# The odd x product of a block, shared by the block's last four steps

## The chip, the cores and the metric

The kernel runs on one core of a Trainium2 chip. The metric is the device time of one execution in microseconds. Three runs of the kernel before gave a median of 1644.59 us (1644.28 to 1645.88).

## What is computed

A gated recurrent layer runs over 512 time steps with a batch of 8 and 512 units, and its states are added to the input. `h0` is a second input; all numbers are float32. The reference, cut to its core:

```python
def step(h, x_t):
    fused = jax.nn.sigmoid(jnp.concatenate([x_t, h], axis=-1) @ w_W + w_b)
    hidden_state, output_state = jnp.split(fused, 2, axis=-1)
    memory_state = x_t @ wx_W + wx_b + hidden_state * (h @ wh_W + wh_b)
    h_new = output_state * h + (1.0 - output_state) * jnp.tanh(memory_state)
    return (h_new, h_new)
_, hs = jax.lax.scan(step, h0, xT)
return x + jnp.swapaxes(hs, 0, 1)
```

Each step has a part that needs the state h (products with 1536 columns of weights in all) and a part that needs x alone (1536 columns too). The second can be computed for many steps at once, ahead of the recurrence.

## The kernel before

**One step of the recurrence.** The 512 steps are one unrolled loop (L469). The state is kept transposed: 128 partitions by four chunks k of 8 columns, in two halves (chunks 0 and 1, chunks 2 and 3). A step's TensorE work is given by `ORDER` (L27): A0 to A3, D0 to D3, H2 and H3. A letter is a bank of PSUM and a slice of weights, the digit the chunk of h that is the stationary operand. `BANKS` (L31) gives the widths of the moving operand, 256, 128 and 64 columns; for chunks 2 and 3, A has 192 columns only (L485). Each of these is four matmuls (L491), one for each group of 32 columns of the array, so that the four run side by side. Each float32 matmul is recorded as two matmul instructions with a weight load each (two passes): D of one step, 4 chunks by 4 groups, is 32 records.

Behind A, VectorE and ScalarE turn the sums into gates and the new state: `turn_r`, `turn_h`, `turn_z`, `memory`, `update` (L594 to L620), for the first half of h first, and then for the second, which also needs D and H. The scans of `update(1, 0)` and `update(1, 1)` (L619, L620) make chunks 2 and 3 of the new state; the next step's A2 and A3 wait for them, while its A0 and A1 need the first half alone.

**The x part.** After the products of a step, TensorE gets some of the x part (L493 to L500). For the first groups of steps these are plain products. From step 14 on they come from `products` (L376), for blocks c = 2 to 31 of 16 steps each: each block's product of x with the weights is made by a scheme of seven by seven smaller products (after Strassen and Winograd), whose operands are sums that GpSimd (x) and VectorE (weights, once) have made. So a block has 49 products, each with 96 columns (`BL`, L35) and again four matmuls side by side. The seven outer stages are worked through in the order of `STAGES`; of a stage, three products go to bank `xps[0]`, four to bank `xps[1]` (`SLOTS`, L41). When a bank's products of a stage are done, VectorE adds them up with `drain` (L390, recorded as L403), and a next stage's products may only be written to that bank behind it. GpSimd puts the results together (`result`, L405).

`products` is a generator that yields after each product, and `take(later, n)` (L420) lets it run for n yields. 49 products in 16 steps is three in each, and one over: the last step of a block takes four (L500). The steps at which the drains are issued are worked out from the same count (L456 to L463), with a product counted as 1.

Of the kernel before, what the change touches and what calls it, by code (L numbers as in the profile page):

```python
# [14 lines left out]
NQ = 4  # L15
# [19 lines left out]
BL = 96  # L35
# [3 lines left out]
FRESH = (2, 5, 1)  # L39

SLOTS = ((1, 6, 7), (2, 3, 4, 5))  # L41

LEAD = 18

PLAIN = (2, 3, 5, 6, 8, 10, 11, 13, 14, 16)

# [8 lines left out]
def tile_cond_rnn_residual(  # L55
# [144 lines left out]
    xps = [psum.tile([P, 512], F32, name=f"xp{q}") for q in range(2)]  # L200

    def mm(out_, lhsT, rhs, start=False):
        nc.tensor.matmul(  # L203
            out_, lhsT, rhs, start=start, stop=False, skip_group_check=True
        )
# [20 lines left out]
    for b in range(2):  # L226
        c0 = COLS.start + BL * b
# [56 lines left out]
    def wx_of(kh, nh):  # L284
        return wx[:, 2 * kh : 2 * kh + 2, :, HALF * nh : HALF * nh + HALF]
# [31 lines left out]
    def x_block(c, r, kh):  # L317

        return xins[c][:, :, 2 * kh : 2 * kh + 2, 32 * r : 32 * r + 32]
# [31 lines left out]
    def x_sums(c):  # L351
        jobs = [(x_sum, c, n) for n in range(4)]
        return jobs + [(inner_x, c, n, p) for n in range(4) for p in (0, 2, 3)]

    def left(c, p, q):

        xr, kh = {1: (0, 0), 2: (0, 1), 4: (1, 1)}.get(p, (None, None))
        at = {1: 0, 2: 1, 4: 2, 5: 3, 6: 4, 7: 5, 3: 6}[p]
        if q in (3, 5, 6, 7):
            return si[c % 2][:, at, {5: 0, 6: 1, 7: 2, 3: 3}[q]]  # L360
        e, k = {1: (0, 0), 2: (0, 1), 4: (1, 1)}[q]
        if xr is None:
            return so[c % 2][:, at - 3, e, k]
        return x_block(c, xr, kh)[:, e, k]

    def right(p, q, j):

        kh, nh = {1: (0, 0), 2: (1, 0), 3: (1, 1)}.get(p, (None, None))
        at = {1: 0, 2: 1, 3: 2, 5: 3, 6: 4, 7: 5, 4: 6}[p]
        if q > 3:  # L370
            return ti[:, at, {5: 0, 6: 1, 7: 2, 4: 3}[q], j]
        k, b = {1: (0, 0), 2: (1, 0), 3: (1, 1)}[q]
        w = tw[:, at - 3] if kh is None else wx_of(kh, nh)
        return w[:, k, j, BL * b : BL * b + BL]

    def products(c):  # L376

        for q in STAGES:
            for bank in range(2):
                for n, p in enumerate(SLOTS[bank]):  # L380
                    for j in range(NQ):
                        mm(
                            xps[bank][32 * j : 32 * j + 32, BL * n : BL * n + BL],
                            left(c, p, q),
                            right(p, q, j),
                            start=q in FRESH and n == 0,
                        )
                    yield

    def drain(q, bank):  # L390

# [28 lines left out]
    def take(it, n=None):  # L420
        while n is None or n > 0:
            if next(it, it) is it:
                return
            n = None if n is None else n - 1

    def x_side():
        for c in range(2, NCH):
            yield from products(c)
# [4 lines left out]
    later = x_side()  # L433
# [12 lines left out]
    def at_step(i, *todo):  # L446
        jobs.setdefault(i, []).extend(todo)
# [4 lines left out]
    for c in range(2, NCH):  # L452
        w0 = TC * c - LEAD
        for n, q in enumerate(x_sums(c)):
            at_step(w0 - (13 if c > 2 else 10) + n // 2, q)
        done = 0  # L456
        for w in range(TC):
            n = done
            done += 3 + w // 15
            for m, q in enumerate(STAGES):  # L460
                for bank in range(2):
                    if n < 7 * m + 3 + 4 * bank <= done:
                        drains.setdefault(w0 + w, []).append((q, bank))  # L463
        for e, w in ((0, 11), (1, 15)):
            for n in range(7):
                at_step(w0 + w + n // 2, (result, e, n))

    pool_done = {}
    for i in range(T):  # L469
        g, s = divmod(i, GS)  # L470
        c, t = divmod(i, TC)
# [6 lines left out]
        for n in (ORDER if i else FIRST).split():  # L478
# [3 lines left out]
            bank, k = n[0], int(n[1])  # L482
# [10 lines left out]
        if 1 <= i < 4:  # L493
            take(first[2], 2 if i == 3 else 3)
        elif i == 0:
            take(first[1], 1)
        elif i < 4 + len(PLAIN):
            take(first[4], PLAIN[i - 4] - (PLAIN[i - 5] if i > 4 else 0))
        else:
            take(later, 4 if (i + LEAD) % TC == TC - 1 else 3)  # L500

        rows = slice(B * s, B * s + B)
        s1 = (i + 1) % GS
# [255 lines left out]
```

## Time and profile before

| what | value |
|---|---|
| three runs, median | 1644.59 us |
| profiled execution, device time | 1642.24 us |
| profiled execution, span of the trace | 1640.4 us |
| granted TensorE clock, mean | 0.999 |
| busy PE, weight load, VectorE, ScalarE, GpSimd | 99%, 83%, 84%, 60%, 34% of the span |

The span runs from the first to the last instruction of the trace. In the profile PE is TensorE's matmuls, PEld its weight loads, which overlap with them, DVE VectorE, ACT ScalarE and POOL GpSimd. A matmul's end is modelled and overlaps with the next, so that starts say more of TensorE than durations do. All matmuls are issued by one helper and carry its line, L203; they are told apart by the tiles they write (A, D, H, xp). In a timeline, neighbouring instructions of a kind are merged into one row with a count, and the brackets give the idle time of that engine ahead of the row and whose work ended it.

### The profile page before, as it was taken

Reading aid. Unit: us, or ns where it says so; the run is one execution under the profiler, and the core shown is the slowest. Engines: PE = TensorE matmul, PEld = TensorE weight load, DVE = VectorE, ACT = ScalarE, POOL = GpSimd, SP = SyncE. Lnnn points to the kernel's source line nnn. Section 1 sums busy time; section 2 is a strip of 40 time slices with the busy share of each in tenths; the row PEclk is TensorE's granted clock in tenths of the full one; section 3 lists DMA queues with packets and bytes.
Section 4 is the critical chain, followed back from the end, with each engine's and each line's share of the span. In section 5 each row is a group of like instructions: output and inputs, shape, how many; then the busy total and the mean of one; then the engine's idle time right before and its main releaser. Section 6 shows DMA issues by size and latency. Waiting matters only on the chain.

```text
span 1640.4 us, 124811 instructions
## 1 busy us (share of the span) xinstructions
PE 1627.4 (99%) x53006; PEld 1362.0 (83%) x53006; DVE 1384.8 (84%) x11239; ACT 977.2 (60%) x5520; POOL 550.3 (34%) x1443
## 2 busy tenths in 40 slices
PE   8999999999999999999999999999999999999998
PEld 5788888888888888888888888888888888888876
DVE  8888888888888888888888888888888888888886
ACT  3666666666555665666566666566666666556655
POOL 3333333333333333333333333333333333333220
PEclk9999999999999999999999999999999999999999
DMA  4000000000000000000000000000000000000000
GB/s 182 17 5 17 18 18 18 5 18 18 18 17 17 5 18 18 17 18 5 17 18 18 17 10 14 17 18 18 18 5 18 17 18 17 5 17 12 11 11 10
DMA packets 11512, 31.08 MB, mean 19 GB/s; under 512 B 1220, under 2 KB 1732, under 8 KB 10952
## 3 DMA queue, kind: packets, MB, share of 16 engines
q1 hardware_dynamic: 10800, 22.94, 4.1%
q8 instruction: 414, 6.78, 1.7%
q14 instruction: 146, 1.20, 0.2%
q10 hardware_dynamic: 152, 0.16, 0.0%
HBM read 14.70 MB, written 8.39 MB: 14 GB/s over the span
## 4 chain that ended last, share of the span: by engine, by line
PE 97%; DVE 1%; DMA 1%; issue 0%; SPq 0%; ACT 0%; DVEq 0%
PE A L203 48%; PE D L203 26%; PE xp L203 16%; PE H L203 7%; DMA wd<-in_wd_dram 1%; DVE tr L519 0%; DVE m L507 0%; DMA head<-in_xh_dram 0%; DVE md1B L576 0%; DVE md1A L534 0%; DVE tz L519 0%; DVE hT L507 0%; SPq L142 0%; ACT hT L243 0%; DVE idle L542 0%
## 5 line engine op out<-in xcount | busy, mean ns | idle before, releaser
L203 PE MATMUL A<-wa,hT 128*32 128x256 f32 x16352 | 884.7, 356 | 4.1 <-DVE hT L507 4.1
L203 PEld LDWEIGHTS A<-wa,hT 128*32 128x32 f32 x16352 | 509.5, 123 | 236.2 <-DVE hT L507 133.6
L203 PE MATMUL D<-wd,hT 128*32 128x128 f32 x16384 | 543.0, 273 | 1.0 <-DMA wd<-in_wd_dram 1.0
L203 PEld LDWEIGHTS D<-wd,hT 128*32 128x32 f32 x16384 | 482.7, 122 | 21.8 <-DMA wd<-in_wd_dram 1.3
L673 POOL TENSOR_TENSOR ot<-xin,hT 128x32 f32<-128x32 f32 x503 | 136.0, 270 | 1048.4 <-DVE hT L507 1036.9
L243 ACT ACTIVATE hT<-m 128x8 f32<-128x8 f32 x2048 | 324.1, 207 | 91.5 <-DVE m L507 91.3
L243 ACT ACTIVATE md0A<-tr 128x16 f32<-128x16 f32 x512 | 112.8, 220 | 409.5 <-DVE tr L519 409.5
L519 DVE STREAM_TRANSPOSE tr<-A 128x64 f32<-128x64 f32 x511 | 127.7, 250 | 221.1 <-PE A L203 221.0
L243 ACT ACTIVATE hT<-hT 128x16 f32<-128x16 f32 x1024 | 233.3, 228 | 85.0 <-DVE hT L507 84.2
L203 PE MATMUL H<-wa,hT 128*32 128x64 f32 x8208 | 210.5, 219 | 0.0
L203 PEld LDWEIGHTS H<-wa,hT 128*32 128x32 f32 x8208 | 187.8, 122 | 0.1
L507 DVE TENSOR_TENSOR_SCAN hT<-hd0B,hT 128x24 f32<-128x24 f32 x1024 | 154.5, 192 | 21.8
L507 DVE TENSOR_TENSOR_SCAN hT<-hd0A,hT 128x24 f32<-128x24 f32 x1024 | 171.6, 168 | 0.0
L507 DVE TENSOR_TENSOR_SCAN m<-md0B,md1B 128x24 f32<-128x24 f32 x1024 | 154.6, 193 | 0.0
L203 PE MATMUL xp<-ti,si 128*32 128x96 f32 x5040 | 150.0, 246 | 0.0
L507 DVE TENSOR_TENSOR_SCAN m<-md0A,md1A 128x16 f32<-128x16 f32 x1024 | 142.2, 181 | 5.0
L243 ACT ACTIVATE md0B<-tr 128x16 f32<-128x16 f32 x512 | 116.2, 227 | 42.8 <-DVE tr L519 1.3
L418 POOL TENSOR_TENSOR xs<-ff 128x192 f32<-128x192 f32 x240 | 141.0, 599 | 0.0
L576 DVE STREAM_TRANSPOSE md1B<-A 128x64 f32<-128x64 f32 x511 | 130.1, 255 | 0.0
L243 ACT ACTIVATE hd0A<-tz 128x16 f32<-128x16 f32 x512 | 116.5, 228 | 21.5
L534 DVE STREAM_TRANSPOSE md1B<-H 128x64 f32<-128x64 f32 x512 | 128.2, 250 | 0.1
L569 DVE STREAM_TRANSPOSE hd0B<-sz 128x64 f32<-128x64 f32 x512 | 126.3, 247 | 0.0
(103 smaller groups left out, 1919.8 us busy)
## 6 DMA issues: line engine op xcount, KB each, us to landing
xin<-in_x_dram SPq DMA_DIRECT2D x31, 256.0 KB, 3.2
out_dram<-ot SPq DMA_DIRECT2D x31, 256.0 KB, 2.3
wx<-in_wx_dram SPq DMA_DIRECT2D x4, 768.0 KB, 6.9
wa<-in_wa_dram SPq DMA_DIRECT2D x4, 512.0 KB, 9.6
wd<-in_wd_dram SPq DMA_DIRECT2D x1, 768.0 KB
wd<-in_wd_dram SPq DMA_DIRECT2D x1, 256.0 KB, 11.2
out_dram<-ot SPq DMA_DIRECT2D x1, 192.0 KB, 1.9
head<-in_xh_dram ACTq DMA_DIRECT2D x1, 144.0 KB, 4.9
```

The source lines that it names most:

```text
L203: nc.tensor.matmul(out_, lhsT, rhs, start=start, stop=False, skip_group_check=True)
L243: inst = nc.scalar.activation(out_, in_, func, **kw).ins
L418: nc.gpsimd.tensor_tensor(to, a, b, ALU.add)
L507: return nc.vector.tensor_tensor_scan(*[t_[:, :, c_].rearrange("p n c s -> p (n c s)") for t_ in (out_, d0, d1)], 0.0, ALU.mult, ALU.add,).ins
L519: inst = nc.vector.transpose(t_.rearrange("p c n -> p (c n)"), raw[n][hf]).ins
L534: inst = nc.vector.transpose(md1[hf][g % 2][:, :, :, hf].rearrange("p n c -> p c n"), raw["h"][hf]).ins
L569: inst = nc.vector.transpose(hd0[1][i % 2][:, :, :, 2].rearrange("p n c -> p c n"), sz).ins
L576: nc.vector.transpose(md1[1][g % 2][:, :, :, 0].rearrange("p n c -> p c n"), ps["A"][:, :HU])
L673: pool_done[i + 1] = nc.gpsimd.tensor_tensor(ot[:, t], x_of(c, slice(0, NQ), t, 1), hTs[(i + 1) % NH][:, :, :, B * s1 : B * s1 + B, 2].rea ...
```

## The change

The x work of a step is counted in columns, not in products. `BURSTS` gives the columns of a block's 16 steps: 288 (three products) in twelve of them and 312 in the last four. `products` cuts a product at the end of a step's share: it runs the four matmuls on the first columns, yields, and runs them again on the rest in the next step, with the same stationary operand. The drains' steps are worked out in columns, and each step takes one yield.

```diff
+BURSTS = (288,) * 12 + (312,) * 4
...
     def products(c):
+        todo = list(BURSTS)
         for q in STAGES:
             for bank in range(2):
                 for n, p in enumerate(SLOTS[bank]):
-                    for j in range(NQ):
-                        mm(
-                            xps[bank][32 * j : 32 * j + 32, BL * n : BL * n + BL],
-                            left(c, p, q),
-                            right(p, q, j),
-                            start=q in FRESH and n == 0,
-                        )
-                    yield
+                    c0 = 0
+                    while c0 < BL:
+                        c1 = min(BL, c0 + todo[0])
+                        for j in range(NQ):
+                            mm(
+                                xps[bank][32 * j : 32 * j + 32, BL * n + c0 : BL * n + c1],
+                                left(c, p, q),
+                                right(p, q, j)[:, c0:c1],
+                                start=q in FRESH and n == 0 and c0 == 0,
+                            )
+                        todo[0] -= c1 - c0
+                        c0 = c1
+                        if not todo[0]:
+                            todo.pop(0)
+                            yield
...
-            done += 3 + w // 15
+            done += BURSTS[w]
...
-                    if n < 7 * m + 3 + 4 * bank <= done:
+                    if n < BL * (7 * m + 3 + 4 * bank) <= done:
...
-            take(later, 4 if (i + LEAD) % TC == TC - 1 else 3)
+            take(later, 1)
```

## The prediction

> **What bounds the kernel now.** I read the page first: span, engines, and the chain that ended last.
>
> ```profile
> span 1640.4 us, 124811 instructions
> ...
> PE 1627.4 (99%) x53006; PEld 1362.0 (83%) x53006; DVE 1384.8 (84%) x11239; ACT 977.2 (60%) x5520; POOL 550.3 (34%) x1443
> ...
> PE 97%; DVE 1%; DMA 1%; issue 0%; SPq 0%; ACT 0%; DVEq 0%
> ...
> L403 DVE TENSOR_TENSOR ff<-xp,off x60: 429/482/535, 117.1 to 1580.9; 128x288 f32<-128x288 f32 x30, 128x384 f32<-128x384 f32 x30
> ```
>
> The page makes PE look like the bound (99% busy, 97% of the chain). That cannot be taken at its word, since ends of matmuls are modelled and overlap. The last line is from the view of the tile xp: the last stage of a block is drained once from each bank, 30 times, so 30 blocks have the four-product step that the change removes.
>
> The next view is the weight loader's timeline over a block's last steps (columns: start, duration, engine, what, count, idle before it and who ended it).
>
> ```profile
> 781.79 0.96 PEld L203 LDWEIGHTS D<-wd,hT 128*32 128x32 f32 x32
> ...
> 818.87 0.51 PEld L203 LDWEIGHTS A<-wa,hT 128*32 128x32 f32 x16 [0.27 <-DVE hT L507]
> 819.41 0.96 PEld L203 LDWEIGHTS D<-wd,hT 128*32 128x32 f32 x32
> 820.34 0.36 PEld L203 LDWEIGHTS H<-wa,hT 128*32 128x32 f32 x16
> 820.61 0.18 PEld L203 LDWEIGHTS xp<-ti,xin 128*32 128x32 f32 x8
> 820.75 0.38 PEld L203 LDWEIGHTS xp<-ti,so 128*32 128x32 f32 x16
> 821.09 0.64 PEld L203 LDWEIGHTS A<-wa,hT 128*32 128x32 f32 x16
> 822.01 0.51 PEld L203 LDWEIGHTS A<-wa,hT 128*32 128x32 f32 x16 [0.27 <-DVE hT L507]
> 822.54 0.96 PEld L203 LDWEIGHTS D<-wd,hT 128*32 128x32 f32 x32
> ...
> 824.38 1.41 PEld L203 LDWEIGHTS A<-wa,hT 128*32 128x32 f32 x32
> 825.81 0.96 PEld L203 LDWEIGHTS D<-wd,hT 128*32 128x32 f32 x32
> ...
> 828.41 0.51 PEld L203 LDWEIGHTS A<-wa,hT 128*32 128x32 f32 x16 [0.27 <-DVE hT L507]
> ```
>
> In a step with three products, A is loaded in two halves: the second (chunks 2 and 3, A2 and A3 below) waits for VectorE's scan that makes the second half of h. In the step with four products (A at 824.38) there are 32 loads in a row and no wait. So the three-product steps are bound by the recurrence, and the four-product step by PE. From D at 781.79 to D at 822.54 lie 13 three-product steps: 40.75/13 = 3.135 us each. From D at 822.54 to 825.81 is the four-product step: 3.27 us. The odd product thus costs 0.135 us, and all 30 together 30 x 0.135 = 4.05 us: the most that the change can give back.
>
> That three products are free is also seen at the end of the kernel, where no x product is left:
>
> ```profile
> 1586.46 0.62 PEld L203 LDWEIGHTS A<-wa,hT 128*32 128x32 f32 x16 [0.39 <-DVE hT L507]
> 1587.37 0.51 PEld L203 LDWEIGHTS A<-wa,hT 128*32 128x32 f32 x16 [0.29 <-DVE hT L507]
> ...
> 1608.36 0.62 PEld L203 LDWEIGHTS A<-wa,hT 128*32 128x32 f32 x16 [0.39 <-DVE hT L507]
> ```
>
> Seven steps from 1586.46 to 1608.36 take 21.90/7 = 3.129 us each: no x product at all, and the same step to within 0.006 us.
>
> Last, PE's own timeline, for what a product costs and how much room a step has.
>
> ```profile
> 818.03 1.72 PE L203 MATMUL A<-wa,hT 128*32 128x256 f32 x32
> 819.57 1.05 PE L203 MATMUL D<-wd,hT 128*32 128x128 f32 x32
> 820.44 0.40 PE L203 MATMUL H<-wa,hT 128*32 128x64 f32 x16
> 820.67 0.35 PE L203 MATMUL xp<-ti,xin 128*32 128x96 f32 x8
> 820.83 0.51 PE L203 MATMUL xp<-ti,so 128*32 128x96 f32 x16
> 821.16 1.72 PE L203 MATMUL A<-wa,hT 128*32 128x256 f32 x32
> 822.70 1.05 PE L203 MATMUL D<-wd,hT 128*32 128x128 f32 x32
> 823.57 0.41 PE L203 MATMUL H<-wa,hT 128*32 128x64 f32 x16
> 823.80 0.35 PE L203 MATMUL xp<-ti,xin 128*32 128x96 f32 x8
> ...
> 824.46 1.70 PE L203 MATMUL A<-wa,hT 128*32 128x256 f32 x32
> 825.97 1.05 PE L203 MATMUL D<-wd,hT 128*32 128x128 f32 x32
> ```
>
> Starts, not durations, are to be read. Four products take 824.46 - 823.80 = 0.66 us, 0.165 us each. A product is four matmuls side by side in column groups, and each is recorded as two passes (x8), so a pass of 96 columns takes 0.0825 us. Without waiting, A takes 825.97 - 824.46 = 1.51 us for four passes of 256 and four of 192 columns: 0.843 ns a column. D (819.57 to 820.44, eight passes of 128) gives 0.85, H (820.44 to 820.67, four passes of 64) 0.23/4 = 0.057 a pass, about 0.055 by the columns. A pass costs its columns, down to 64; nothing narrower runs in this kernel.
>
> The room in a step: A takes 1.54 us where it waits (818.03 to 819.57, 821.16 to 822.70) and 1.51 where it doesn't, so 0.03 us; the other way, the odd product costs 0.135 of its 0.165 us, so 0.030 us. This room decides the case.
>
> **The change part by part.**
>
> *Removed:* the fourth product of the 16th step, 0.165 us of PE, of which 0.135 us showed: 30 x 0.135 = -4.05 us.
>
> *Added:* 24 columns in each of the last four steps. The columns are the same in all; the pieces are not. Product 40 is cut 24/72, product 43 48/48, product 46 72/24. So step 13 runs three products and a piece of 24; step 14 72 + 96 + 96 + 48; step 15 48 + 96 + 96 + 72; step 16 24 and three products. Three more groups of four matmuls, thus 24 passes and 24 weight loads by the records' count, in each block, 720 of each in all.
>
> By columns alone 24 columns cost 0.165/4 = 0.041 us. But each pass also needs its own weights, and the two timelines show when these are loaded. D's first load starts 0.16 us ahead of its first matmul (819.41, 819.57), which is one A pass of 192 columns; H's 0.10 ahead (820.34, 820.44), one D pass; xp's 0.06 ahead (820.61, 820.67), one H pass; A's 0.07 ahead (821.09, 821.16), one xp pass. So a load goes out when the pass before it starts, one pass ahead and no more. How long does it need? The stall at A2 tells. A0 and A1 are 1024 columns, 0.863 us, so PE is free at 821.16 + 0.863 = 822.02. The 768 columns of A2 and A3 take 0.647 us, so they started at 822.70 - 0.647 = 822.05. Their load started at 822.01: 0.043 us from load to matmul. The step before gives 818.92 - 818.87 = 0.05. I take 0.043 us, the figure of the row read with less rounding, as the least time of a pass: a pass of 24 columns (0.021 us) can't be followed by the next before 0.043 us, one of 48 (0.041) barely not, one of 72 (0.062) isn't touched.
>
> Pieces of two passes, then: 24 columns 0.086, 48 columns 0.086, 72 columns 0.124 us. PE's time beyond three products: step 13 0.086; step 14 0.124 + 0.086 - 0.165 = 0.045; step 15 the same 0.045; step 16 0.086. Less the room of 0.030: 0.056 + 0.015 + 0.015 + 0.056 = 0.142 us a block, 30 x 0.142 = +4.26 us.
>
> The price of a short pass isn't in the trace, so both ends. Below: columns alone, four steps of 0.041 - 0.030 = 0.011, 0.045 a block, +1.35 us, net -2.7. Above: no narrow pass under H's 0.057 us, so 0.114 for 24 and for 48 columns: 0.084 + 0.043 + 0.043 + 0.084 = 0.254 a block, +7.6 us, net +3.6. A price above the 64-column row is excluded by that row as far as weights go, since H's loads are hidden behind its own passes. The 0.043 is nearest, because it is the same unit doing the same load.
>
> The Trainium skill speaks to the load too ("TensorE: Matmul & The Clock Gate", section "LDWEIGHTS (loading the stationary operand)"): a load takes about its columns over 1.2 in ns, 27 ns for these 32 columns. By it, an estimate, 24 columns would cost 0.054 and the block 0.072 us, net -1.9 us; the row says 0.043 us from load to matmul, and I go by the row.
>
> *Moved, at no cost:* product 43's first half runs a step earlier in bank 0 and product 46's first part a step earlier in bank 1, and each now waits itself for VectorE's drain of the stage before.
>
> ```profile
> 818.84 0.53 DVE L403 TENSOR_TENSOR ff<-xp,ee 128x384 f32<-128x384 f32 x1
> ...
> 819.82 0.25 DVE L519 STREAM_TRANSPOSE tr<-A 128x64 f32<-128x64 f32 x1 [0.31 <-PE A L203]
> ```
>
> The drain of bank 1 ends at 819.37, and the step's x products start at 820.67: 1.3 us to spare. What stands behind that matmul on PE is the next step's A; without the cover it would be late by the drain's 0.53 us at most. The drains themselves stay at their steps: the block's boundaries 38, 42, 45 and 49 fall in the same steps under 288 and 312 columns as under 3 and 4 products. VectorE, which carries the recurrence, ScalarE, GpSimd and SP issue the same in the same order; and VectorE still sits idle for PE's A (0.31 us even behind a drain). No DMA is moved. Delaying A0 by 0.05 us costs nothing else: A0 and A1 need the first half of h, for which the load at 821.09 doesn't wait.
>
> *Sum:* -4.05 + 4.26 = +0.2 us, on the profiled execution's 1640.40 us of span and 1642.24 us in all (1.84 us around the span): 1640.6 and 1642.4. The median of the runs shown lies 2.35 us higher, 1644.59; so 1644.8 us.
>
> **The rivals.**
>
> *A, short passes cost their columns* (the weights of a short pass come early enough, as the 0.043 us at the stall is partly the wake-up from a wait and not the load). For it: every pass down to 64 columns follows its columns. Against: each load is seen to go out only as the pass before starts. Net -2.7 us: 1641.9; halfway, with a least pass of 0.03 us, 0.060 for 24 columns: 0.030 + 0.012 + 0.012 + 0.030 = 0.084, net -1.5: 1643.1.
>
> *B, slower: a short pass costs what a 64-column pass costs.* Place: the four steps' pieces of 24 and 48 columns; price: 0.057 us a pass, net +3.6 us, 1648.2. It decides from a least pass above 0.043 us, where what is added outgrows what was removed. For it: H's passes, the narrowest here, are the only row of a narrow matmul, and the loader can't be seen to be any faster under load. Against: H follows its columns, which a floor would hide only if it lay just there. The Trainium skill has the rule that speaks for it ("TensorEngine Tiling (Array Packing)", section "Instruction Overhead"): a matmul has some 60 cycles of overhead, so that one column takes as long as 60. No run here shows it; read as 60 columns a pass, an estimate, it gives 0.101 us for 24 and 48 columns and net +2 us.
>
> *C, the pieces vanish wholly*: the room is larger than read, as where PE waits for h it can be filled. Then all 4.05 us are saved, 1640.5. Against: 24 columns alone are 0.041 us, over the 0.030 of room by two readings.
>
> *D, the change doesn't do what it says*: the step of 3.27 us stays, because something else than PE holds it. Against: its A has no wait. Then only the pieces' cost is left in three steps, +2.6 us, 1647.2.
>
> **How the numbers follow.** The forecast 0.48 (own range 1643.8 to 1645.9: 0.01 us of rounding in the least pass is some 0.04 us a block, 1.2 us in all); A 0.26; B 0.20; C 0.03; D 0.03. What a measurement of this kernel can tell from no change is about 0.2%, 3.3 us: 1641.3 to 1647.9. Faster needs C, or A with luck: 0.04. Slower is B's upper half and a price that no row shows: 0.13. Within: 0.83. The range leaves out C, a bit of A and the upper half of B: 1642.1 to 1648.0.
>
> **What would show it.** The steps 13 to 16 of a block, by starts of D: I expect 3.19, 3.15, 3.15, 3.19 us, in place of 3.135 three times and 3.27. A: four times 3.145. B: 3.22, 3.18, 3.18, 3.22. In all four the 32 loads of A should run without a wait, and the weight loader's rows for 24 columns should stand 0.043 us apart. Starts of the pass after a 24-column pass settle the least pass at once. Wrong would be any of the other twelve steps changing from 3.135, or a wait of PE for a drain in step 14 or 15.

## The result and the profile after

The changed kernel takes 1649.18 us (median of 9 runs, 1646.65 to 1653.98), the kernel before, in as many runs beside it, 1643.43 us (1642.32 to 1645.88). The ratio is 1.0039, with a 95% interval of 1.0031 to 1.0047: 0.4% slower, clear of the noise, and outside the range that was forecast. The changed kernel's runs also scatter over 7.3 us, those of before over 3.6.

The page of the changed kernel, its span, its engines and the queue that carries instructions (packets, MB, share of the DMA engines):

```profile
span 1648.2 us, 126251 instructions
...
PE 1633.5 (99%) x53726; PEld 1380.8 (84%) x53726; DVE 1385.7 (84%) x11239; ACT 976.8 (59%) x5520; POOL 548.9 (33%) x1443
...
q8 instruction: 420, 6.88, 1.7%
```

The same row of the page of before:

```profile
q8 instruction: 414, 6.78, 1.7%
```

The 720 matmuls and 720 weight loads more are there. VectorE and the others do what they did. By its count the queue q8 brings PE's own program: 53726 matmuls and as many weight loads are 107452 instructions, over 420 packets 255.8 each. So a packet is 256 instructions, and the 1440 added ones are six packets more.

Now the four steps at the end of a block, in the weight loader's timeline of the changed kernel (start, duration, what, count, idle before). First a block in which nothing else happens:

```profile
716.23 0.96 PEld L205 LDWEIGHTS D<-wd,hT 128*32 128x32 f32 x32
...
717.43 0.69 PEld L205 LDWEIGHTS xp<-ti,si 128*32 128x32 f32 x32
718.01 0.62 PEld L205 LDWEIGHTS A<-wa,hT 128*32 128x32 f32 x16
718.83 0.56 PEld L205 LDWEIGHTS A<-wa,hT 128*32 128x32 f32 x16 [0.19 <-DVE hT L517]
719.41 0.96 PEld L205 LDWEIGHTS D<-wd,hT 128*32 128x32 f32 x32
...
722.01 0.54 PEld L205 LDWEIGHTS A<-wa,hT 128*32 128x32 f32 x16 [0.22 <-DVE hT L517]
722.56 0.97 PEld L205 LDWEIGHTS D<-wd,hT 128*32 128x32 f32 x32
...
725.16 0.53 PEld L205 LDWEIGHTS A<-wa,hT 128*32 128x32 f32 x16 [0.22 <-DVE hT L517]
725.71 0.97 PEld L205 LDWEIGHTS D<-wd,hT 128*32 128x32 f32 x32
...
728.31 0.56 PEld L205 LDWEIGHTS A<-wa,hT 128*32 128x32 f32 x16 [0.20 <-DVE hT L517]
728.88 0.15 PEld L205 LDWEIGHTS D<-wd,hT 128*32 128x32 f32 x4
```

From D to D: 3.18, 3.15, 3.15, 3.17 us. The forecast was 3.19, 3.15, 3.15, 3.19. Here the steps are as long as they were reckoned to be, or a little shorter. In a block two later it looks otherwise:

```profile
823.81 0.96 PEld L205 LDWEIGHTS D<-wd,hT 128*32 128x32 f32 x32
...
825.01 0.18 PEld L205 LDWEIGHTS xp<-ti,xin 128*32 128x32 f32 x7
825.36 0.11 PEld L205 LDWEIGHTS xp<-ti,xin 128*32 128x32 f32 x1 [0.17 <-issue]
...
827.20 0.98 PEld L205 LDWEIGHTS D<-wd,hT 128*32 128x32 f32 x32
...
828.61 0.20 PEld L205 LDWEIGHTS xp<-ti,xin 128*32 128x32 f32 x7
829.11 0.11 PEld L205 LDWEIGHTS xp<-ti,xin 128*32 128x32 f32 x1 [0.30 <-issue]
...
830.66 1.02 PEld L205 LDWEIGHTS D<-wd,hT 128*32 128x32 f32 x32
```

Here two steps take 3.39 and 3.46 us in place of 3.15 and 3.17. In both a row of x products is torn after the seventh of a product's eight loads, in the middle of a group of four, with an idle time that ends by "issue": no semaphore, nothing that the profile shows. The view of waits, cut to the blocks from 100 to 1500 us (line, waited for: us in total, times, longest), says how often. The kernel before:

```profile
PEld xp L203 <- issue: 0.5, 2, 0.3
PEld A L203 <- issue: 0.5, 2, 0.3
```

The changed kernel:

```profile
PEld xp L205 <- issue: 4.4, 15, 0.5
PEld A L205 <- issue: 0.6, 3, 0.3
PEld D L205 <- issue: 0.3, 1, 0.3
PEld H L205 <- issue: 0.2, 1, 0.2
```

The view counts only what the loader lost beyond its usual gaps. For the whole loss I took the start of one VectorE transpose that runs once a step (hd0B<-sz), hence the length of every step, and for each of a block's 16 places the median over the 30 blocks. The sum of the 16 medians is 50.271 us before and 50.265 us after: by regular steps alone, the change gains 30 x 0.006 = 0.2 us. What lies above the medians, called irregular time from here on, adds up to 2.8 us before and 10.6 us after. The 7.8 us by which the profiled span grew (1640.4 to 1648.2) come from these irregular stops.

They also have a place. If all matmuls and loads that started before a stop are counted, then of 19 gaps of over 0.235 us between starts of matmuls within the blocks, 18 stand at instruction 193 or 194 of 256, though the tiles differ (A, D, H and all x products). A stop at one place in every 256 instructions, in a program that is delivered in packets of 256, led to theory 1: PE has run out of instructions and waits for the next packet. The rival: the narrow pieces (their passes of few columns), or the two new waits for drains, cost it.

### The profile page after: what moved, and what is told of

Read it like the earlier page. It is cut to its first block, busy times and chain, and to the rows that moved or that the text cites. A ratio compares the mean times of both kernels' runs of the same rounds, so it can differ in the third digit from the quotient of the medians.

```text
span 1648.2 us, 126251 instructions
## 1 busy us (share of the span) xinstructions
PE 1633.5 (99%) x53726; PEld 1380.8 (84%) x53726; DVE 1385.7 (84%) x11239; ACT 976.8 (59%) x5520; POOL 548.9 (33%) x1443
## 4 chain that ended last, share of the span: by engine, by line
PE 97%; DVE 1%; DMA 1%; issue 0%; SPq 0%; ACT 0%; DVEq 0%
PE A L205 48%; PE D L205 26%; PE xp L205 16%; PE H L205 7%; DMA wd<-in_wd_dram 1%; DVE tr L529 0%; DVE m L517 0%; DMA head<-in_xh_dram 0%; DVE md1B L586 0%; DVE md1A L544 0%; DVE tz L529 0%; DVE hT L517 0%; SPq L144 0%; ACT hT L245 0%; DVE idle L552 0%
## 5 line engine op out<-in xcount | busy, mean ns | idle before, releaser
L205 PEld LDWEIGHTS A<-wa,hT 128*32 128x32 f32 x16352 | 523.5, 123 | 221.4 <-DVE hT L517 128.0
L205 PE MATMUL H<-wa,hT 128*32 128x64 f32 x8208 | 214.7, 219 | 0.1
L205 PEld LDWEIGHTS H<-wa,hT 128*32 128x32 f32 x8208 | 191.6, 122 | 0.4 <-issue 0.2
L205 PE MATMUL xp<-ti,si 128*32 128x96 f32 (+2 forms) x5280 | 153.0, 243 | 0.8 <-issue 0.5
```

Of the source, the lines that this page charges most:

```text
L205: nc.tensor.matmul(out_, lhsT, rhs, start=start, stop=False, skip_group_check=True)
```

## The experiments

All times of a group come from the same chip as the runs of the kernel before beside them. The added instructions are counted per step: a step with three products has 208 on PE (104 matmuls, as many loads), one with four products, or with three and a cut, 224.

**Instructions without columns.** The columns of every step are those of before; four products of a block are cut into two halves of 48 columns. Against the changed kernel:

```diff
-BURSTS = (288,) * 12 + (312,) * 4
+BURSTS = (288,) * 15 + (384,)
+CUTS = (12, 13, 14, 15)
...
                         c1 = min(BL, c0 + todo[0])
+                        w = len(BURSTS) - len(todo)
+                        if w in CUTS and BURSTS[w] - todo[0] < BL:
+                            c1 = min(c1, c0 + BL // 2)
```

> The columns of each step are those of the kernel before (288, in the 16th step 384); the first whole product of steps 13 to 16 is cut into two pieces of 48 columns, so that 16 instructions more run on PE in each of these steps (64 a block; the change has 48). Theory 1, instruction fetch: PE's instructions arrive in packets of 256, and a stretch of steps with 224 in 3.13 us outruns them; the stalls of the changed kernel come here without its share of columns: 5 to 12 us slower than before. Rival, narrow passes: a pass of 48 columns is just at the 0.043 us from load to matmul, so nothing is added: within 0.8 us of before.

Measured: 1653.08 us, before 1643.50; ratio 1.0057 (1.0043 to 1.0071), 9.6 us slower. The regular steps didn't grow: their medians sum to 50.290 us a block, 0.02 more than before, which is 0.6 us in all. What lies above the medians is 15.0 us in the profiled run (1655.34 us). So a kernel with the columns of before is slowed by 16 instructions more in each of four steps.

The second has `CUTS = (3, 7, 11, 15)`.

> As the kernel before, with the first product of steps 4, 8, 12 and 16 cut into two of 48 columns: the same 64 more instructions a block, but three steps with 208 between two with 224. Theory 1 with the rate over some steps as what counts: fewer stalls than with the four cuts in a row, 0 to 4 us slower than before. If the count alone decides, whatever the place: as slow as with the cuts in a row. Rival, narrow passes: within 0.8 us of before.

Measured: 1651.84 us, ratio 1.0048 (1.0035 to 1.0060), 8.3 us slower; the irregular time of the profiled run (1649.49 us) is 9.4 us. The rival falls again. So does the guess that the rate over several steps counts: with quiet steps in between the loss is nearly as large, and the two intervals overlap. A quiet step saves up little or nothing for the next one.

**Fewer cuts.** The odd product in two halves, one cut a block:

```diff
-BURSTS = (288,) * 12 + (312,) * 4
+BURSTS = (288,) * 14 + (336,) * 2
```

> The odd product is shared by the last two steps, 336 columns each: one cut, 16 instructions more a block than before in place of 48. By the columns each of the two steps is 0.053 us longer and the 3.27 us step is gone: 0.03 us a block, 0.9 us faster than before. Theory 1, instruction fetch: a third of the changed kernel's stalls at most is left, so between 1 us faster and 3 us slower than before. Rival, that the new waits of PE for the drains do it: one of the two waits is left, so half of the change's loss, 3 us slower.

Measured: 1644.72 us, ratio 1.0010 (1.0001 to 1.0019), 1.2 us slower. By its regular steps (medians sum to 50.243 us) it gains 0.8 us; the irregular ones, 5.2 us against 2.8, take more. Between the kernels in loss as in instructions, and no gain.

**The odd product left out.** `BURSTS = (288,) * 16`, with the 49th product never run and its drain kept.

> The 49th product of each block is left out, so that all 16 steps have 288 columns and 208 PE instructions; nothing else is changed. It measures what the odd product costs in all. By the starts in the trace 30 x 0.137 = 4.1 us faster than before on every theory; theory 1 adds that some of the few stalls of before go as well, so 4 to 6.5 us faster.

Measured: 1636.89 us, ratio 0.9960 (0.9948 to 0.9973), 6.6 us faster, just over what was expected. The medians fall by 0.132 us a block, 4.0 us, as the 0.135 us of the prediction have it. The rest, 2.6 us, isn't settled: in this profiled run the irregular stops are 2.9 us, as many as before, and the profiled runs of the kernel before and of this one, 1642.24 and 1638.08 us, lie 4.2 us apart. The rest lies in runs of which no profile was kept.

**How fast instructions come.** Half the columns of each x product are left out, which gives PE room. Then zero, one, two or three of three products are cut in two pieces of 24, which adds instructions and no columns. (The 16th step of a block, with its fourth product, has 16 instructions more than the others without cuts and 32 more with them.) Against the kernel before:

```diff
+CUT = 3
...
-                    for j in range(NQ):
-                        mm(
-                            xps[bank][32 * j : 32 * j + 32, BL * n : BL * n + BL],
...
+                    turn = (turn + 1) % 3
+                    step = BL // 4 if turn < CUT else BL // 2
+                    for c0 in range(0, BL // 2, step):
+                        for j in range(NQ):
+                            mm(
+                                xps[bank][32 * j : 32 * j + 32, BL * n + c0 : BL * n + c0 + step],
...
```

> Half the columns of every x product are left out (48 of 96), so that PE has some 0.27 us of room in each step; instructions are as in the kernel before, 208 a step. Reference for the next three. All theories: the recurrence alone sets the step, and the four-product step is covered: 4 to 6 us faster than before, 1637 to 1640 us.

> As the one with half the columns, and one product of each step in two pieces of 24: the same columns, 224 PE instructions a step. Theory 1, instruction fetch: 256 instructions in 3.58 us, about where the changed kernel begins to stall: 10 to 80 us slower than the one without cuts. Rival, narrow passes: the room covers them, no change within 2 us.

> As the one with half the columns, two products of each step in two pieces of 24: 240 PE instructions a step. Theory 1: 256 instructions would have to arrive in 3.34 us; if a packet takes some 3.6 us from request to request, the step becomes 3.4 us: 60 to 150 us slower than the one without cuts. Rival, narrow passes: the room covers them (0.086 us each at most), no change within 3 us.

> As the one with half the columns, all three products of each step in two pieces of 24: 256 PE instructions a step, one packet. Theory 1: the step becomes as long as a packet takes, 3.5 to 3.8 us: 170 to 300 us slower than the one without cuts, and the length of the step is the fetch's own rate. Rival, narrow passes: six pieces of 0.086 us are 0.52 us where three products of 0.165 and the room of 0.03 were, so within 5 us of the one without cuts.

Measured:

| PE instructions in a step | time | more than without cuts |
|---|---|---|
| 208 | 1635.17 us | |
| 224 | 1681.24 us | 46 us |
| 240 | 1785.56 us | 150 us |
| 256 | 1896.19 us | 261 us |

The kernel before took 1640.69 us beside them (ratios 0.9963, 1.0241, 1.0877, 1.1550; interval of the last 1.1490 to 1.1611). The rival gave each of them less than 5 us. The packets that q8 brought between 100 and 1500 us, in the view of the DMA queues, with 240 instructions a step:

```profile
q8 instruction: 384, 6.29, 1.8%
```

With 256 instructions a step:

```profile
q8 instruction: 385, 6.31, 1.9%
```

1400 us over 384 and 385 packets are 3.65 and 3.64 us a packet; with 224 instructions there were 383, 3.66 us. Whether a step has 224, 240 or 256 instructions, no more than one packet in 3.65 us comes. In the same stretch the kernel before took 363 packets, one in 3.86 us, and the changed kernel 367, one in 3.81. How this shows on PE is seen in the weight loader's timeline of the kernel with 256 a step:

```profile
837.44 0.20 PEld L205 LDWEIGHTS A<-wa,hT 128*32 128x32 f32 x8
838.55 0.94 PEld L205 LDWEIGHTS A<-wa,hT 128*32 128x32 f32 x24 [0.90 <-DVE hT L513]
...
840.44 0.36 PEld L205 LDWEIGHTS H<-wa,hT 128*32 128x32 f32 x16
...
841.19 0.20 PEld L205 LDWEIGHTS A<-wa,hT 128*32 128x32 f32 x8
842.29 0.94 PEld L205 LDWEIGHTS A<-wa,hT 128*32 128x32 f32 x24 [0.90 <-DVE idle L658]
```

With one packet a step the edge, where one packet's instructions end and the next one's begin, falls at the same place in a block's steps, here after the first eight loads of A. By the count that was used above, 335 of 351 gaps of over 0.235 us between 100 and 1500 us stand at instruction 193 or 194 of 256. The releaser that the profile names isn't the cause there: in the kernel before, A's first sixteen loads stand in one row without a wait, with the same semaphores. The profile names the last one that it can find. Nor is it that PE takes no more than one instruction in 3.65 us/256 = 14 ns: the 64 loads and 64 matmuls of H and the x products start between 840.44 and 841.19, 6 ns each.

The records of the q8 packets show more when they are set against these edges (the start of the instruction behind the 194th of each 256). Both in the kernel before and in the one with 256 a step, exactly one packet starts between each edge and the next from 100 to 1500 us: 363 and 385 times. In the means it starts 0.70 us (before) and 1.17 us (256 a step) after the edge, takes 1.07 and 1.09 us, and has landed 2.09 and 1.39 us ahead of the next edge, which adds up to the 3.86 and 3.65 us. So the transfer is under a third of the limit. And the packets keep close behind the edges: all 363 of the kernel before start 0.0 to 1.7 us after one, none in the later half of the 3.86 us between two. That PE's passing the edge sets the next packet off would explain why quiet steps save up nothing; the order shows it as possible, not as shown.

The rate sorts the other runs, in an estimate that takes each step by itself. A step with 208 instructions needs 208/256 x 3.65 = 2.97 us, one with 224 needs 3.19, one with 240 needs 3.42. Before, 208 have 3.135 us and 224 have 3.27: enough. The four changed steps have 224 in 3.18, 3.15, 3.15 and 3.17 us by their columns: all a little short, 0.11 us together, 3.3 us over 30 blocks. With four cuts in steps of unchanged columns, three steps are short by 0.055 and one by 0.15, 0.315 us, 9.5 us in all, in a row or apart: 9.6 and 8.3 were measured. The closeness is partly luck: by the same estimate the changed kernel should lose 3.3 us less its gain, and it loses 5.75, and the kernel before should lose nothing, and has 2.8. Scatter of the packets near the limit would do that, and an estimate from a mean rate gives the least; it isn't shown.

**The undoing.** Everything of the change stays, cuts, narrow pieces and waits; but steps 13 to 16 have 16 other instructions less at equal columns. The kernel leaves out the products H2 and H3 there, so that its states are not the layer's, and runs one product of as many columns that is not read:

```diff
+            if bank == "H" and 14 <= i < 494 and (i + LEAD) % TC >= 12:
+                if k == 2:
+                    for j in range(NQ):
+                        mm(xps[0][32 * j : 32 * j + 32, 384:512], hs, wa[:, k, j, :128])
+                continue
```

> The changed kernel, but in steps 13 to 16 of a block the products H2 and H3 (two of 64 columns) are left out and one product of 128 columns into unused columns of bank 0 runs in their place: PE streams as many columns, with 16 instructions less, so that these steps have 208 in place of 224. The cuts, the narrow pieces and the new waits for drains stay. Theory 1, instruction fetch: the loss of the change goes, and its own merit of 0.5 us may show: 1641 to 1644.5 us, 0 to 2.5 us faster than before. Rival, that the narrow pieces or the waits themselves cost it: 1648 to 1650 us as the changed kernel.

Measured: 1638.42 us beside 1640.52 of before; ratio 0.9985 (0.9977 to 0.9994), 2.1 us faster. The 5.75 us of loss are gone, and a gain is there (part of it is the exchange's own, see below). The medians of its steps sum to 50.235 us and what lies above them is 0.3 us. A block's end at its weight loader:

```profile
811.49 0.96 PEld L205 LDWEIGHTS D<-wd,hT 128*32 128x32 f32 x32
812.41 0.25 PEld L205 LDWEIGHTS xp<-wa,hT 128*32 128x32 f32 x8
812.63 0.73 PEld L205 LDWEIGHTS xp<-ti,si 128*32 128x32 f32 x32
...
814.66 0.96 PEld L205 LDWEIGHTS D<-wd,hT 128*32 128x32 f32 x32
...
817.81 0.96 PEld L205 LDWEIGHTS D<-wd,hT 128*32 128x32 f32 x32
...
820.95 0.96 PEld L205 LDWEIGHTS D<-wd,hT 128*32 128x32 f32 x32
```

The eight loads "xp<-wa,hT" are the exchanged product. The steps are 3.17, 3.15 and 3.14 us, with the same 32 loads of x products in the first of them as in the changed kernel; and its view of waits between 100 and 1500 us has no row that ends by issue.

The same exchange in all steps of the blocks, once for the changed kernel and once for the kernel before (condition `14 <= i < 494`):

> The changed kernel with that exchange in all steps of the blocks (H2 and H3 left out for one product of 128 columns elsewhere): 192 PE instructions in twelve steps of a block and 208 in four, the same columns. Theory 1: no fetch stalls worth naming are left, so the time is the recurrence and the change's four longer steps: 1639.5 to 1642 us, and 0 to 1.5 us faster than the kernel before with the same exchange. Rival: slower than that one by 5 us or more.

> The kernel before with that exchange in all steps of the blocks (H2 and H3 left out for one product of 128 columns elsewhere): 192 PE instructions in fifteen steps and 208 in the 16th, the same columns. Theory 1: the few irregular long steps of before, some 2.5 us in its trace, go: 1 to 3 us faster than before. Rival: no change.

Measured: 1638.05 us and 1639.30 us, beside 1640.52; ratios 0.9985 (0.9976 to 0.9993) and 0.9992 (0.9983 to 1.0001). With fewer instructions than the packets can bring, irregular time is 0.2 and 0.4 us, and the change is worth 1.25 us, near the 0.03 us a block (0.9 us) by which the sums of medians differ (50.219 and 50.250). All times of this group lie lower than expected in absolute terms because the kernel before ran at 1640.52 on that chip; the differences are as expected.

## Why the prediction was wrong

**The bound now:** right. The recurrence holds the three-product steps at 3.13 us and PE the fourth product's; the odd product costs 0.135 us (0.132 when left out).

**Removed, and added by columns and loads:** right in kind, and a little too dear. In the changed kernel's own PE timeline a step with three products and a piece of 24 columns reads

```profile
818.73 0.73 PE L205 MATMUL xp<-ti,si 128*32 128x96 f32 x32
819.29 1.71 PE L205 MATMUL A<-wa,hT 128*32 128x256 f32 x32
```

0.56 us less 3 x 0.165 leaves 0.065 us for the piece (the row names only the first of its shapes). In the medians over the 30 blocks, the x products of the four steps take 0.060, 0.045, 0.045 and 0.063 us more than three products; the prediction had 0.086, 0.045, 0.045 and 0.086, and columns alone are 0.041. So a narrow pass does take longer than its columns, some 0.03 us and not 0.043: the halfway point of rival A. That the weight load holds it isn't shown: the four matmuls of a pass start 0.007 us apart, which makes 0.03 us too. Rival B, 0.057 a pass, is out, and so is the reading of the overhead rule as 60 columns a pass (0.05 us). The forecast's own range was reckoned too narrow upward: 0.01 us more in the least pass adds 0.02 us to each of the four steps, 0.08 a block and 2.4 us, not 0.04 and 1.2.

**The signs:** the lengths of the four steps came to within 0.02 us, but A's 32 loads don't run without a wait. In the quiet block above the loader still waits 0.19 to 0.22 us for h. PE is hardly held by it: from A to D it takes 1.53, 1.51, 1.51 and 1.51 us behind these four steps (medians over the 30 blocks), 1.54 behind the others. The room of 0.03 us is used up, as reckoned.

**Moved, at no cost:** right. The waits for drains, VectorE and the drains' steps stayed as they were, and the undone kernel has all of them and is faster than before.

**The step that failed** is the one that counted "720 of each in all" and priced these matmuls and loads by their passes alone. As instructions they were given no price. By the regular steps the sum is right, 0.2 us less where it had 0.2 more; the missing term is the irregular stops, 7.8 us more in the profiled runs. The same part closed with the sentence that no DMA is moved, but the program itself comes by DMA, 256 instructions a packet, and the page had the queue in its third part. What stood in the trace of before: 106012 instructions of PE in 414 packets, one in 3.86 us in the blocks, and a step of 224 instructions only where it had 3.27 us. What did not stand there is the limit, 3.65 us, 5% below that use. The prediction asked whether a short pass fits between two loads, and not whether its instruction fits between two packets. Rival B's 1648.2 us stands near the 1649.18 by luck: its sign was right, its mechanism wasn't. PE streamed about as forecast, and stood still elsewhere. "Any of the other twelve steps changing from 3.135" was named as what would be wrong, and it is what happened: their medians stayed, but 6.6 of the 10.6 us of irregular time fall in them (before, 2.2 of 2.8), since the stops fall wherever a packet ends.

The Trainium skill ("Runtime: NRT & Kernel Launch", section "Instruction fetch mechanics") says that an engine's program is refilled in blocks of 16 KiB, 256 instructions, over a queue of the sequencer's own, and that the cost of crossing a block is mostly hidden. The packets of q8 agree with the block. On the cost, the runs here say otherwise for PE in a kernel of small matmuls: hidden up to about one block in 3.65 us, and 46 to 261 us beyond.

Open: what the 2.56 us of the limit are spent on in which no packet is under way, whether other DMA traffic moves it, and where the further 2.6 us in the run without the odd product come from. A kernel that keeps all its work and saves 16 PE instructions in these four steps would be the one to beat both, by at most the 2 us that the undone one shows (1.2 us of them come with the exchange in the kernel before, too); it wasn't tried, as each way that I found puts columns ahead of a wait of VectorE.

## What to carry to other kernels

Where a matmul is cut to balance time, count instructions per microsecond as well as columns: here a matmul and a weight load for each recorded pass, and 256 in 3.65 us as the most that PE was given. Read the instruction queue's packets against the span before adding any, and look for idle time that ends by "issue" in the middle of a group. Spreading work in smaller pieces can lose more by the cutting than the balance gains.

## What the runs showed of the hardware

PE's program comes no faster than 256 instructions in 3.64 to 3.66 us, at 224, 240 and 256 instructions a step alike, while all queues together take about 5% of the DMA engines' time. A packet's own transfer takes 1.09 us of it in the mean, with 256 a step. In the kernel with 256 a step the steps are not evenly long: mostly about 3.47 or 3.74 us, some 4.02, so 0.27 us apart, as if the arrival were looked for at intervals, which no run here shows. And a fetch hardly works ahead: three quiet steps between two dense ones saved 1.3 of 9.6 us at most, which the intervals don't tell from none, and in the kernel before all 363 packets start only when PE has passed an edge, 0.0 to 1.7 us behind it.
